# Four-layer graph network on one core: two attentions begin in another order, and the diffusion of the second is shared out as 30 and 24 products a period

## The chip, the cores and the metric

One Trainium2 chip, one core. The metric is the device time of one execution in microseconds, from the median of several runs. TensorE (PE) multiplies matrices and transposes, VectorE (DVE), ScalarE (ACT) and GpSimd (POOL) do the elementwise work and the reductions, and SyncE (SP) issues the transfers. Each engine takes its instructions in order from its own queue; they wait for each other by semaphores.

## The reference, cut to what matters

The input is `x` (3327 x 256) and a sparse weighted `adj` (3327 x 3327). Four layers follow each other, each ending in a residual and a layer norm. The change touches the last one alone:

```
def _top_p_attention(X, W1, W2, W3):
    logits = (X @ W1.T @ W2.T) @ (X @ W3.T).T
    probs = softmax(logits)
    # of each row keep the largest entries whose preceding sum is under 0.9, scale them to sum 1
    ...
R = (S + eye) / rowsum
for n in range(2):
    A  = _top_p_attention(Xa, W1, W2, W3)
    Xf = R @ Xf              # "diffusion"
    Xa = A @ Xa              # "attention"
    Z  = Z + Xf @ U1[n].T + Xa @ U2[n].T
out = layernorm(x + layernorm(X + Z))
```

The two steps of the loop are called the first and the second attention here. The second needs the result of the first for all rows, because its keys are made from all of them.

## The kernel before, in words

The rows are padded to 3328 and cut into 26 tiles of 128 (`nt` = 26, `nh` = 13). For each tile `t` of an attention there are these steps:

- `scores` (L1139 to L1164) makes the row of logits in a buffer `e` (128 x 3328). It goes in four groups: two matmuls into the PSUM tile `sc` (two banks, one buffer), then a copy to `e` by ACT. So the next group's matmuls wait for the copy of this one. One column of padding is set by a POOL memset (L1146).
- A search finds the cut of each row. `search_short` (first attention) takes the eight largest of each of 26 segments on DVE (`cand`), subtracts the maximum in an `Exp` on ACT over the whole row, ranks 48 candidates in six rounds, and zeroes what lies under the cut in two half rows (`e<-e,v` with 1664 elements). `search_long` (second attention) runs six passes of ACT over the whole row: an `Exp` at half scale (L1439), the `Exp` itself (L1444), then `Relu` (L1459) and `Sign` (L1461) at a first cut `c1`, and `Relu` (L1477) and `Sign` (L1490) at a second cut `c2`. POOL works out the cuts from the sums between the passes. With the third cut DVE masks each half row (`z`, L1506), takes segment maxima (L1356), ranks them (L1367, L1369), removes ties (L1535) and zeroes the rest in one pass over 3328 elements (L1543).
- `attended` transposes `e` on PE (`tp`, L1330), ACT copies the transposes to `wt`, and PE multiplies them with 26 blocks of `G` or `X` (L1344). For the first attention, `attended_pair` does this for two tiles at once with seven half-width products a block.
- `diffused` (second attention, L1299) multiplies 26 blocks of `adjT`, loaded in pieces `at`, with `Y`; its result `xf` lies in a ring of `DL + 3` = 4 buffers. `diffused_first` and `diffused_pair` do the same for the first attention.
- `first` ends a tile of the first attention: projections, keys and query of the second attention (`store_keys`), and one block of `G`, which is written to DRAM (`gd`) because the memory of `G` is still in use for the first attention's combinations of `X`; later it is read back. `second` ends a tile of the second attention.

In the first attention PE and DVE are held to the program's order. In the second, a scheduler orders PE's and DVE's instructions by what is ready, and ACT's passes and copies keep the program's order. The second attention is written as periods `i`: in period `i` the attention of tile `i - 1` is multiplied, tile `i` is in the last part of its search, `i + 1` in the first, and the scores of `i + 2` are made. Each period also takes a share of the 676 diffusion products:

```
later = (nt - 2) * nt
shares = [later * (k + 1) // (nt - 1) - later * k // (nt - 1) for k in range(nt - 1)]
for i in range(-2, nt + 1):
```

That is 26 in each of the periods -1 and 0, and 24 or 25 in each of the periods 1 to 25.

The first attention begins with the scores of tile 0, one group after each four products of `diffused_first`; the pair diffusion `spreading(1)` is started before tile 1's scores. The second attention begins after the last tile's `first`, in new pools.

Of the kernel before, what the change touches and what calls it, by code (L numbers as in the profile page):

```python
# [18 lines left out]
P = 128  # L19
D = 256  # L20
# [30 lines left out]
def gnn_kernel(ctx: ExitStack, tc: tile.TileContext, n: int, a: dict, out: bass.AP):  # L51
# [816 lines left out]
    with tc.tile_pool(name="l3", bufs=1) as pool, tc.tile_pool(name="l3d", bufs=1, space=DRAM) as dram:  # L868
# [269 lines left out]
        def in_order(op):  # L1138
            return lambda *x, **k: tc.keep_in_program_order(op(*x, **k))  # L1139

        def scores(work, psum, p, q, e):


            copy = in_order(nc.scalar.copy) if p else nc.scalar.copy
            if npad > n:
                nc.gpsimd.memset(e[:, n:], NEG)  # L1146
            halves = e.rearrange("p (h c) -> p h c", h=2)
            for c0 in range(0, half, KC):
                pl = psum.tile([P, 2, 512], F32, name="sc", bufs=1)
                ws = [min(KC, n - c0 - h * half) for h in range(2)]  # L1150

                for h, w in enumerate(ws):
                    k = slice(h * DA, (h + 1) * DA)
                    mm = tensor.matmul(pl[:, h, :w], q[k, :], kT[p][k, c0:c0 + w], start=True, stop=True)  # L1154
# [150 lines left out]
        def diffused(work, atp, psum, p, it, out, each=J3):  # L1305

            rd = rdeg[:, it:it + 1]
            t = work.tile([P, D], F32, name="t")
            nc.gpsimd.tensor_scalar(t, (Y if p else X)[:, it, :], rd, None, op0=ALU.mult)
            if p:  # L1310
                s = work.tile([P, D], F32, name="s")
                nc.sync.dma_start(s, sd[it])
                nc.gpsimd.tensor_tensor(t, t, s, op=ALU.add)
            for acc in aggregated(atp, psum, it, Y if p else X, each):
                if acc is None:
                    yield
            d = work.tile([P, D], F32, name="xf", bufs=DL + 3)
            nc.vector.scalar_tensor_tensor(d, acc, rd, t, op0=ALU.mult, op1=ALU.add)
            out.append(d)

# [100 lines left out]
        junks = [None]  # L1421
        edge = [None]

        def search_long(work, sm, e, total, v, kept, halves=False):

# [1 line left out]

            def t(name):  # L1430
                return t1(sm, name)

            m8, neg, root = t1(sm, "m8", 8), t1(sm, "neg", 2), t("root")
            nc.vector.max(m8, e[:, :KC])
# [22 lines left out]
            f1, sg, k1, m1 = t("fs1"), t("sg"), t("k1"), t("m1")  # L1457
# [3 lines left out]
            here(nc.scalar.activation(junk, e, AF.Sign, bias=c1, scale=-1.0, accum_out=sg))  # L1461
# [19 lines left out]
            with tc.issue_after(second_cut.ins):  # L1481
# [8 lines left out]
            here(nc.scalar.activation(junk, e, AF.Sign, bias=c2, scale=-1.0, accum_out=sg))  # L1490
            yield
            x, c3 = t("x"), t("c3")
            nc.vector.reciprocal(s, s)
# [59 lines left out]
        def first(work, psum, it, acc, f, xf, tag="pj", xa=None):  # L1553

            xa = work.tile([P, D], F32, name="h") if xa is None else xa
            nc.scalar.mul(xa, acc, f)
            yield
            pt = psum.tile([P, 4, P], F32, name=tag)
            for i, v in enumerate((xf, xa)):
                for k in range(2):  # L1560
                    tensor.transpose(pt[:, 2 * i + k, :], v[:, k * P:(k + 1) * P], ident)
            xt = work.tile([P, 4, P], F32, name="xt", bufs=1)
            vector.tensor_copy(xt, pt)
            yield
            ps = psum.tile([P, 4, P], F32, name=tag).rearrange("p (k x) d -> p k (x d)", k=2)
            for k in range(4):
                tensor.matmul(ps[:, 0, :], xt[:, k, :], (u1 if k < 2 else u2)[:, 0, k % 2, :], start=(k == 0), stop=(k == 3))
            for k in range(2):
                tensor.matmul(ps[:, 1, :], xt[:, k, :], u1[:, 1, k, :], start=(k == 0), stop=(k == 1))
            nc.scalar.copy(Y[:, it, :], ps[:, 1, :])  # L1570
            yield
            s = work.tile([P, D], F32, name="s")
            vector.tensor_add(s, ps[:, 0, :], X[:, it, :])
            nc.sync.dma_start(sd[it], s)
            pg = psum.tile([P, 4, P], F32, name=tag).rearrange("p (k x) d -> p k (x d)", k=2)
            for k in range(2):
                tensor.matmul(pg[:, 0, :], xt[:, 2 + k, :], u2[:, 1, k, :], start=(k == 0), stop=(k == 1))
            project_keys(pg[:, 1, :P], it, xt[:, 2:, :])
            g = G[:, it, :] if tag == "pj" else work.tile([P, D], F32, name="s")
            nc.scalar.copy(g, pg[:, 0, :])  # L1580
            if tag != "pj":
                nc.sync.dma_start(gd[it], g)
            store_keys(work, pg[:, 1, :P], 1, it)
            yield
# [70 lines left out]
        with tc.tile_pool(name="l3w", bufs=2) as work, tc.tile_pool(name="l3s", bufs=4) as sm:  # L1655


            def start(p, t, es, searches, search):
                if p or t:
                    q = work.tile([2 * DA, P], F32, name="q")  # L1660
                    nc.sync.dma_start(q, qd[p][t])
                else:
                    q = q0
                es[t] = work.tile([P, npad], F32, name="e", bufs=4)
                searches[t] = search(work, sm, es[t], *(x[p][:, t:t + 1] for x in (tots, vs, kepts)),
                                     **({"halves": True} if p and t == nt - 1 else {}))
                return scores(work, psum, p, q, es[t])

            with tc.tile_pool(name="l3p", bufs=2, space=PSUM) as psum, tc.tile_pool(name="l3a", bufs=1) as quads:
                fixed = True  # L1670
# [56 lines left out]
                        next(todo[r][0])  # L1727
                    ends[0] = todo[0][0]

                groups = logits(0)  # L1730
                x = diffused_first(quads, psum, 1, xfs)
                for _ in groups:
                    next(x)
                queue.append(searches[0])
                spread = spreading(1)
                groups = logits(1)
                for _ in x:
                    next(groups, None)
                    looks(2)
                for _ in groups:  # L1740
                    pass
                queue.append(searches[1])
# [2 lines left out]
                for i in range(nh - 1):  # L1745
                    stage(spread, 7, logits(2 * i + 2), ends, counts,
                          {0: lambda: end_pair(i - 1) if i else None, 5: lambda: attend_to(i), 6: go_on})
                    go_on()
                    counts = [1, 2, 2, 2, 2, 0, 0]
                    queue.append(searches[2 * i + 2])  # L1750
                    values = turned[0]
                    for k in range(7):
                        next(values)
                        looks(k in (1, 2, 4, 5, 6))
                    stage(spread, 6, logits(2 * i + 3), todo[1], [2, 1, 2, 1, 2, 1], {})
                    finish()
# [14 lines left out]
                for it in (nt - 2, nt - 1):  # L1771
# [14 lines left out]
                        pass  # L1786
                    ends = first(quads, psum, it, acc, f, xfs[it], "tp", c)
                    next(ends)
                both(ends)
                fl0 = unresolved(sm, psum, 0)  # L1790
                fixed = False
            for x in (slice(0, JH), slice(JH, nt)):
                nc.sync.dma_start(G[:, x, :], gd[x].rearrange("t p d -> p t d"))

            with tc.tile_pool(name="l3q", bufs=3, space=PSUM) as psum, tc.tile_pool(name="l3at", bufs=3) as atp, \
                    tc.tile_pool(name="l3b", bufs=2) as lone:
                es, searches, xfs = {}, {}, []  # L1800
                result = iter(())
                spread = (x for j in range(nt) for x in diffused(lone, atp, psum, 1, j, xfs, 1))
                later = (nt - 2) * nt
                shares = [later * (k + 1) // (nt - 1) - later * k // (nt - 1) for k in range(nt - 1)]
                for i in range(-2, nt + 1):
                    def search(t):
                        if 0 <= t < nt:
                            next(searches[t])
# [6 lines left out]
                    share = iter(range(shares[i - 1] if 0 < i < nt else nt if -2 < i < 1 else 0))  # L1815

                    def diffuse(products):
                        for _ in range(products):
# [192 lines left out]
```

## Time and profile before

| | us |
|---|---|
| median of 3 runs (3396.72 to 3399.24) | 3396.89 |
| the profiled execution, its own time | 3392.58 |
| its span | 3390.8 |
| busy: PE / DVE / ACT / POOL | 3121.1 / 2692.5 / 1730.8 / 1133.6 |
| first attention's scores begin / second attention's scores begin | 1697.9 / 2547.7 |
| first transposes of the second attention's tile 0 | 2617.1 |

The profiled execution is 1.8 us longer than its span and 4.3 us shorter than the median. "Busy" is an engine's time in instructions; a busy PE is not a PE at its peak. A row of the timeline gives the start in us from the span's start, the duration, engine, line, operation, output and inputs with their shapes, how often in sequence, and in square brackets how long the engine stood idle before it and what ended that.

### The profile page before, as it was taken

The page shows a single profiled execution, that of the slowest core. Times are in us where ns is not written, and L with a number is a line of the kernel's source. Part 1 is how long each engine was busy: PE and PEld are TensorE (multiplying, and loading weights), DVE is VectorE, ACT ScalarE, POOL GpSimd, SP SyncE. Part 2 cuts the span into 40 slices and gives each one's busy share as a digit, 9 for nine tenths or more (in the row PEclk, how much of TensorE's full clock was granted, in tenths as well). Part 3 has the DMA queues.
Part 4 walks back from the last instruction along what each step waited for, and adds up shares of the span by engine and source line. Part 5 has one row for each costly group of instructions (what it writes and reads, how often), then busy time and mean ns, then how long its engine had stood idle before and what let it go on. Part 6 is the DMA issues. An engine that isn't in the chain of part 4 may idle for free. (4 is left out here: it accounts for less than half of the span.)

```text
span 3390.8 us, 50286 instructions
## 1 busy us (share of the span) xinstructions
PE 3121.1 (92%) x18301; PEld 2560.0 (75%) x18301; DVE 2692.5 (79%) x5899; ACT 1730.8 (51%) x2763; POOL 1133.6 (33%) x1328
## 2 busy tenths in 40 slices
PE   8999888988888766999979999999997899999997
PEld 5999656666676555888858898898885677777776
DVE  4665268999999998777578878878854899999996
ACT  1000556767667676111133433433436888888883
POOL 0000245656666655111220000000003566666663
PEclk9999999998999888999989999999998999999999
DMA  6775334333343221444322322322313122222221
GB/s 200 250 257 191 112 98 121 114 108 110 103 118 98 63 61 46 167 143 151 118 79 85 89 73 81 89 73 81 89 41 108 42 68 69 66 59 73 72 63 35
DMA packets 206264, 344.31 MB, mean 102 GB/s; under 512 B 22222, under 2 KB 129166, under 8 KB 205870
## 3 DMA queue, kind: packets, MB, share of 16 engines
q1 hardware_dynamic: 205998, 340.92, 33.1%
q8 instruction: 148, 2.42, 0.3%
q14 instruction: 118, 0.97, 0.1%
HBM read 304.65 MB, written 36.21 MB: 101 GB/s over the span
## 5 line engine op out<-in xcount | busy, mean ns | idle before, releaser
L330 POOL TENSOR_TENSOR h<-du,row 128x2048 f32<-128x2048 f32 (+1 forms) x110 | 465.9, 4235 | 344.7 <-DVE hc L330 243.0
L330 DVE TENSOR_TENSOR_SCAN h<-dA,carry,h 128x512 f32<-128x512 f32 (+1 forms) x384 | 448.8, 1221 | 21.7 <-ACT dA L337 21.5
L337 ACT ACTIVATE dA<-t,A_log 128x512 f32<-128x512 f32 (+1 forms) x448 | 292.6, 658 | 147.7 <-DVE h L330 146.0
L1299 PE MATMUL acc<-F,at 128*128 128x256 f32 x1352 | 345.4, 384 | 3.0 <-DMA at<-in_adjT 2.1
L1344 PE MATMUL acc<-G,wt 128*128 128x256 f32 x1352 | 332.6, 388 | 8.6 <-ACT wt L1139 8.3
L1079 PE MATMUL acc<-F,at 128*128 128x257 f32 x1352 | 302.1, 380 | 0.8 <-ACT r L1023 0.8
L389 PE MATMUL cb<-F,at 128*128 128x256 f32 x1196 | 293.0, 393 | 7.6 <-ACT hn L409 3.4
L1344 PEld LDWEIGHTS acc<-G,wt 128*128 128x128 f32 x1352 | 248.9, 191 | 65.3 <-ACT wt L1139 35.5
L1299 PEld LDWEIGHTS acc<-F,at 128*128 128x128 f32 x1352 | 241.8, 191 | 53.6 <-issue 21.5
L1079 PEld LDWEIGHTS acc<-F,at 128*128 128x128 f32 x1352 | 252.4, 190 | 36.1 <-issue 1.1
L680 PE MATMUL y<-ident,hc 128*128 128x128 f32 x1664 | 235.9, 296 | 45.7 <-DVE hc L330 45.5
L1146 POOL MEMSET e<- 128x1 f32 x52 | 4.9, 99 | 816.2 <-PE tp L891 752.5
L680 PEld LDWEIGHTS y<-ident,hc 128*128 128x128 f32 x1664 | 209.4, 153 | 86.6 <-DVE hc L330 62.1
L389 PEld LDWEIGHTS cb<-F,at 128*128 128x128 f32 x1196 | 228.7, 197 | 58.8 <-issue 20.4
L330 DVE TENSOR_TENSOR hc<-h,row 128x2048 f32<-128x2048 f32 (+2 forms) x114 | 243.0, 2133 | 9.7 <-PE y L680 2.6
L891 PE MATMUL acc<-X,at 128*128 128x128 f32 (+1 forms) x988 | 173.7, 287 | 6.1 <-issue 6.1
L1263 ACT COPY wt<-tp 128x512 f32<-128x512 f32 x156 | 90.7, 591 | 167.1 <-PE tp L891 151.7
L138 PE MATMUL acc<-t,cb 128*128 128x128 f32 (+1 forms) x1014 | 168.4, 275 | 0.0
L891 PEld LDWEIGHTS acc<-X,at 128*128 128x128 f32 x988 | 142.3, 194 | 30.1 <-issue 25.3
L891 PE MATMUL acc<-G,sw 128*128 128x128 f32 x936 | 155.5, 275 | 0.0
L1160 ACT COPY e<-sc 128x832 f32<-128x832 f32 x78 | 65.9, 845 | 174.8 <-PE sc L891 174.7
L891 DVE MAX8 cand<-e 128x8 f32<-128x128 f32 x676 | 139.8, 278 | 5.5 <-ACT e L1160 3.7
(417 smaller groups left out, 7273.0 us busy)
## 6 DMA issues: line engine op xcount, KB each, us to landing
at<-in_adjT SPq DMA_DIRECT2D x54, 832.0 KB, 4.4
at<-in_adjT SPq DMA_DIRECT2D x130, 320.0 KB, 3.0
row<-bc SPq DMA_DIRECT2D x80, 512.0 KB, 4.9
at<-in_adjT SPq DMA_DIRECT2D x52, 640.0 KB, 5.3
at<-in_adjT SPq DMA_DIRECT2D x52, 576.0 KB, 4.3
at<-in_adjT SPq DMA_DIRECT2D x72, 256.0 KB, 3.1
at<-mixed SPq DMA_DIRECT2D x72, 256.0 KB, 3.6
mixed<-cb SPq DMA_DIRECT2D x26, 640.0 KB, 3.9
```

The lines of the kernel that those rows point to most:

```text
L138: mm = nc.tensor.matmul(acc, w[:, j, :], x, start=(y == 0 and k % 3 == 0 and k < 6), stop=(y == nh - 1 and k in (2, 6)))
L330: return lambda *x, **k: tc.keep_in_program_order(op(*x, **k))
L337: decays.append(op(*x, **k))
L389: ten.matmul(acc, at[:, j % JC, :], X0[:, j, :], start=(j == 0), stop=(j == nt - 1))
L680: x = ten.matmul(y[:, g * P:(g + 1) * P], h[:, g, i * P:(i + 1) * P], ident, is_transpose=True, start=(first and g == 0), stop=(last and g ...
L891: return lambda *x, **k: tc.keep_in_program_order(op(*x, **k))
L1079: nc.tensor.matmul(acc, at[:, j, :], F[:, j0 + j, :], start=(j0 + j == 0), stop=(j0 + j == nt - 1))
L1146: nc.gpsimd.memset(e[:, n:], NEG)
L1160: copy(halves[:, :, c0:c0 + ws[0]], pl[:, :, :ws[0]])
L1263: nc.scalar.copy(wts[-1], pt)
L1299: nc.tensor.matmul(acc, at[:, j, :], rhs[:, j0 + j, :], start=(j0 + j == 0), stop=(j0 + j == nt - 1))
L1344: tensor.matmul(acc, wt[:, j, :], rhs[:, j0 + j, :], start=(j0 + j == 0), stop=(j0 + j == nt - 1))
```

## The change

It has five parts.

1. Beginning of the first attention. `scores` may use several PSUM tiles in turn: for tile 0 these are `sc` and one of the `acc` buffers. All four groups of tile 0 come ahead of `diffused_first`. Tile 1's scores are interleaved with `diffused_first` at every second step, with three looks at the search in each step. `spreading(1)` comes after that loop. A one-element ACT copy `ex` is added.
2. End of the first attention. The last four tiles' blocks of `G` are written straight into `G`. The other 22 are read back before the last pair's ends, no longer after all.
3. Beginning of the second attention. The scores of tile 0 are made inside the last `first`, two steps in each of its three. An explicit list of steps for tiles 0 and 1 takes the place of periods -2 and -1.
4. Tile 0 of the second attention is `counted`: its two `Sign` passes on ACT become four `tensor_scalar` passes over half rows on DVE (`is_gt`, summed), two for each cut, with an addition and a rescaling of one column.
5. The shares of diffusion become 30 products in each of periods 1 to 4 and 24 in each of periods 5 to 25. The ring of `xf` has 5 buffers.

```diff
-            for c0 in range(0, half, KC):
-                pl = psum.tile([P, 2, 512], F32, name="sc", bufs=1)
+            for k, c0 in enumerate(range(0, half, KC)):
+                bank = banks[k % len(banks)]
+                pl = psum.tile([P, 2, 512], F32, name=bank, bufs=1 if bank == "sc" else 2)
...
-            d = work.tile([P, D], F32, name="xf", bufs=DL + 3)
+            d = work.tile([P, D], F32, name="xf", bufs=DL + 4)
...
+            def signs(c):
+                ks, sg = t1(sm, "ks", 2), t("sg")
+                if counted:
+                    for h in range(2):
+                        z = lone.tile([P, half], F32, name="z", bufs=1)
+                        nc.vector.tensor_scalar(z, e[:, h * half:(h + 1) * half], c, 0.0, op0=ALU.is_gt, op1=ALU.add,
+                                                accum_out=ks[:, h:h + 1])
+                    nc.vector.tensor_add(sg, ks[:, :1], ks[:, 1:])
+                    nc.vector.tensor_scalar(sg, sg, -2.0, float(npad), op0=ALU.mult, op1=ALU.add)
+                else:
+                    here(nc.scalar.activation(junk, e, AF.Sign, bias=c, scale=-1.0, accum_out=sg))
+                return sg
...
-            g = G[:, it, :] if tag == "pj" else work.tile([P, D], F32, name="s")
+            direct = tag == "pj" or it >= nt - 4
+            g = G[:, it, :] if direct else work.tile([P, D], F32, name="s")
...
-                groups = logits(0)
+                nc.scalar.copy(small.tile([P, 1], F32, name="ex"), eps_t)
                 x = diffused_first(quads, psum, 1, xfs)
-                for _ in groups:
-                    next(x)
+                for _ in logits(0):
+                    pass
                 queue.append(searches[0])
+                groups = logits(1)
+                for k, _ in enumerate(x):
+                    if k % 2 == 0:
+                        next(groups, None)
+                    looks(3)
                 spread = spreading(1)
-                groups = logits(1)
-                for _ in x:
-                    next(groups, None)
-                    looks(2)
...
+                for x in (slice(0, JH), slice(JH, nt - 4)):
+                    nc.sync.dma_start(G[:, x, :], gd[x].rearrange("t p d -> p t d"))
                 end_pair(nh - 2)
...
-                both(ends)
+                es, searches = {}, {}
+                groups = start(1, 0, es, searches, search_long)
+                for _ in ends:
+                    next(groups)
+                    next(groups)
+                both(groups)
...
-            for x in (slice(0, JH), slice(JH, nt)):
-                nc.sync.dma_start(G[:, x, :], gd[x].rearrange("t p d -> p t d"))
...
-                later = (nt - 2) * nt
-                shares = [later * (k + 1) // (nt - 1) - later * k // (nt - 1) for k in range(nt - 1)]
-                for i in range(-2, nt + 1):
+                later, tail = (nt - 2) * nt - 4 * (nt + 4), nt - 5
+                shares = 4 * [nt + 4] + [later * (k + 1) // tail - later * k // tail for k in range(tail)]
+                groups = start(1, 1, es, searches, search_long)
+                for t, products in ((0, 0), (0, 0), (None, 0), (None, 4), (0, 0), (None, 0), (None, 4),
+                                    (0, 0), (0, 0), (None, 0), (None, 4), (0, 0), (None, 0), (None, 4),
+                                    (0, 0), (1, 0), (1, 4), (0, 0), (0, 6)):
+                    next(groups if t is None else searches[t], None)
+                    for _ in range(products):
+                        next(spread)
+                for i in range(nt + 1):
```

More of the change, by code (lines that the diff above doesn't have):

```diff
@@ L1139, in in_order, with scores @@
             return lambda *x, **k: tc.keep_in_program_order(op(*x, **k))
-        def scores(work, psum, p, q, e):
+        def scores(work, psum, p, q, e, banks=("sc",)):
             copy = in_order(nc.scalar.copy) if p else nc.scalar.copy
@@ L1422, in gnn_kernel, with search_long @@
         edge = [None]
-        def search_long(work, sm, e, total, v, kept, halves=False):
+        def search_long(work, sm, e, total, v, kept, halves=False, counted=False):
             def t(name):
                 return t1(sm, name)
+            def signs(c):
[10 more added lines that the diff above has]
+                return sg
             m8, neg, root = t1(sm, "m8", 8), t1(sm, "neg", 2), t("root")
@@ L1456, in search_long @@
             inverse(rc, c1)
-            f1, sg, k1, m1 = t("fs1"), t("sg"), t("k1"), t("m1")
+            f1, k1, m1 = t("fs1"), t("k1"), t("m1")
             yield
@@ L1460, in search_long @@
             yield
-            here(nc.scalar.activation(junk, e, AF.Sign, bias=c1, scale=-1.0, accum_out=sg))
+            sg = signs(c1)
             yield
@@ L1489, in search_long @@
                 scaled(level, c2, float(npad), level, ALU.mult, ALU.add)
-            here(nc.scalar.activation(junk, e, AF.Sign, bias=c2, scale=-1.0, accum_out=sg))
+            sg = signs(c2)
             yield
@@ L1578, in first @@
             project_keys(pg[:, 1, :P], it, xt[:, 2:, :])
-            g = G[:, it, :] if tag == "pj" else work.tile([P, D], F32, name="s")
+            direct = tag == "pj" or it >= nt - 4
+            g = G[:, it, :] if direct else work.tile([P, D], F32, name="s")
             nc.scalar.copy(g, pg[:, 0, :])
-            if tag != "pj":
+            if not direct:
                 nc.sync.dma_start(gd[it], g)
@@ L1665, in start @@
                 searches[t] = search(work, sm, es[t], *(x[p][:, t:t + 1] for x in (tots, vs, kepts)),
-                                     **({"halves": True} if p and t == nt - 1 else {}))
-                return scores(work, psum, p, q, es[t])
+                                     **({"halves": t == nt - 1, "counted": t == 0} if p else {}))
+                return scores(work, psum, p, q, es[t], ("sc", "acc") if not p and t == 0 else ("sc",))
             with tc.tile_pool(name="l3p", bufs=2, space=PSUM) as psum, tc.tile_pool(name="l3a", bufs=1) as quads:
@@ L1788, in gnn_kernel @@
                     next(ends)
-                both(ends)
+                es, searches = {}, {}
[4 more added lines that the diff above has]
+                both(groups)
                 fl0 = unresolved(sm, psum, 0)
                 fixed = False
-            for x in (slice(0, JH), slice(JH, nt)):
-                nc.sync.dma_start(G[:, x, :], gd[x].rearrange("t p d -> p t d"))
             with tc.tile_pool(name="l3q", bufs=3, space=PSUM) as psum, tc.tile_pool(name="l3at", bufs=3) as atp, \
                     tc.tile_pool(name="l3b", bufs=2) as lone:
-                es, searches, xfs = {}, {}, []
+                xfs = []
                 result = iter(())
                 spread = (x for j in range(nt) for x in diffused(lone, atp, psum, 1, j, xfs, 1))
-                later = (nt - 2) * nt
-                shares = [later * (k + 1) // (nt - 1) - later * k // (nt - 1) for k in range(nt - 1)]
-                for i in range(-2, nt + 1):
+                later, tail = (nt - 2) * nt - 4 * (nt + 4), nt - 5
[8 more added lines that the diff above has]
+                for i in range(nt + 1):
                     def search(t):
@@ L1814, in gnn_kernel @@
                         logits = start(1, i + 2, es, searches, search_long)
-                    share = iter(range(shares[i - 1] if 0 < i < nt else nt if -2 < i < 1 else 0))
+                    share = iter(range(shares[i - 1] if 0 < i < nt else nt if i < 1 else 0))
                     def diffuse(products):
```

## The prediction, written before the result

> **What bounds the kernel now.** I read the page first: engines' sums, then the 40 slices.
>
> ```profile
> PE 3121.1 (92%) x18301; PEld 2560.0 (75%) x18301; DVE 2692.5 (79%) x5899; ACT 1730.8 (51%) x2763; POOL 1133.6 (33%) x1328
> ...
> PE   8999888988888766999979999999997899999997
> ...
> PEclk9999999998999888999989999999998999999999
> ```
>
> PE is the bound, except in a few slices. Two of the dents are the change's places: the slices about 1700-1780 (a 7) and about 2540-2630 (7, 8). In the table by stage (PE, PEld, DVE, ACT and POOL busy, clock, DMA share, GB/s) they look like this, with two settled stretches below:
>
> ```profile
> 1740.00:1750.00 10.00, 2.58 (x20) 1.81 (x16) 9.20 (x37) 4.23 (x4) 0.00 (x0) 0.88 0.41 123
> 1750.00:1760.00 10.00, 7.35 (x37) 6.10 (x38) 5.91 (x12) 2.54 (x6) 0.00 (x0) 0.60 0.03 8
> 2550.00:2560.00 10.00, 7.08 (x17) 2.08 (x16) 0.25 (x1) 4.83 (x5) 2.84 (x4) 0.50 0.93 315
> 2610.00:2620.00 10.00, 2.90 (x11) 2.50 (x12) 9.89 (x17) 4.08 (x5) 4.43 (x2) 0.56 0.07 27
> ...
> 3220.00:3240.00 20.00, 20.00 (x102) 15.32 (x101) 19.23 (x66) 15.96 (x18) 12.73 (x30) 1.00 0.18 51
> 3240.00:3260.00 20.00, 20.00 (x97) 14.15 (x96) 18.20 (x54) 16.71 (x17) 14.25 (x22) 1.00 0.20 66
> ```
>
> At both starts PE stands still while DVE or ACT searches tile 0; late in the second attention PE is full. So time at the starts is worth its face value, provided PE's order behind them is the same work; in the build it is (from tile 2's scores on in the first attention the orders agree; before the transposes of the second's tile 0 there are 75 products of diffusion instead of 78).
>
> **First attention's start.** The timeline:
>
> ```profile
> 1716.18 0.18 POOL L1146 MEMSET e<- 128x1 f32 x4
> 1720.70 3.07 ACT L1407 ACTIVATE e<-e,neg 128x3328 f32<-128x3328 f32 x1 [3.73 <-DVE neg L891]
> 1726.72 0.49 DVE L891 SCALAR_TENSOR_TENSOR F<-acc,rdeg,F 128x256 f32<-128x256 f32 x1 [5.79 <-PE acc L891]
> 1737.48 5.12 DVE L891 MAX8 cand<-e 128x8 f32<-128x128 f32 x26
> 1751.31 0.45 PE L891 MATMUL tp<-ident,e 128*128 128x128 f32 x1 [8.73 <-DVE e L891]
> ```
>
> Before, three of tile 0's four groups lie behind diffusion products that wait for `at`; `e` is whole at 1717.0, the maxima end at 1720.0, `Exp` runs 1720.7-1723.8. Then DVE stands 5.79 for `diffused_first`, and its in-order queue holds tile 1's maxima and tile 0's cut behind that, so the first transposes wait to 1751.3. After, the four groups in two PSUM tiles need no product: `e` about 1704.3. But the last column of padding comes from POOL's memset, which runs at 1716.18 because POOL works off 23 own-part products first (1690.0-1716.2, unchanged). So 25 maxima are early and the 26th is not: maximum 1716.6, `Exp` 1717.3-1720.6, cut 1723.0-1726.8. The DVE block is thereby covered; tile 1's maxima start at about 1729.6 (-7.9), the pair diffusion at 1728.2, its 12.65 us are unchanged, and transposes come at about 1743 (-8). Without the memset I would have written 11-13.
>
> PE's clock: 1750-1760 was granted 0.60, about 2 us lost over the first products after the wait of 8.73. The Trainium skill ("TensorE: Matmul & The Clock Gate", "Part 1: The HAM clock gate") has the clock fall after an idle window of about 3.4 us; my new waits there are 2.3 and 1.6, so by the rule PE stays warm: gain 10. Against it stands 2550-2560, at 0.50 with no PE wait over 2.3 in or just before it: gain 8 (the whole sum 30 or 28). Taken: **9** (bounds 4-14: no overlap gained beyond the earlier `Exp`, or that plus the whole DVE wait and the clock). The copy `ex` costs nothing and brings nothing: in the build it stands in an earlier layer, and the table load before the first score copy is still there.
>
> **Second attention's start.**
>
> ```profile
> 2547.71 0.97 PE L1154 MATMUL sc<-kT,q 64*128 64x416 f32 x4 [2.28 <-ACT q L907]
> 2554.99 1.75 PE L1154 MATMUL sc<-kT,q 64*128 64x416 f32 x4 [0.95 <-ACT e L1139]
> 2557.79 3.07 ACT L1439 ACTIVATE junk<-e,neg 128x3328 bf16<-128x3328 f32 x1
> 2573.51 3.09 ACT L1461 ACTIVATE junk<-e,c 128x3328 bf16<-128x3328 f32 x1
> 2585.12 3.07 ACT L1490 ACTIVATE junk<-e,c 128x3328 bf16<-128x3328 f32 x1
> 2590.38 1.95 DVE L1506 SCALAR_TENSOR_TENSOR z<-e,c 128x1664 f32<-128x1664 f32 x1
> 2617.10 1.97 PE L1330 MATMUL tp<-ident,e 128*128 128x128 f32 x8 [9.20 <-DVE e L1543]
> 2639.78 3.54 POOL L1447 TENSOR_SCALAR c<-c,more,less 128x2 f32<-128x2 f32 x1
> ```
>
> - Scores earlier: they ran 2547.7-2556.7, about 2.7 us a group. Three groups move into the last `first`, whose PE waits cover them; the fourth needs the last keys (copied to 2547.4) and ends about 2549. First `Exp` 2550.0 instead of 2557.8: **-7.8**. The last four blocks of `G` skip their DRAM write; L1580 waited 2.33 for one, part of this.
> - Read-back of `G` (1.66 MB), issued at 2548.94 ahead of the `at` loads, moves before the last pair's ends. In SP's queue it then stands behind the 22 writes that it needs, and the last pair's stores and the loads of `s` and `at` stand behind it: if a write were late, these would be too, by some 2-3 us (the `at` loads land 3-5 us after their issue). I take nothing, since those 22 blocks were written tens of us before. PE waits for the read-back only in tile 0's attention, 40 us later. `at` lands at about 2553.8; first products were at 2559.4.
> - Two `Sign` passes (3.07 and about 0.19 for the sum, each) leave ACT's queue; with tile 0 alone they were on the chain (Relu, Sign, POOL, Relu, Sign). Four DVE passes of 1664 run beside `Relu`. Nearest row: the 1664-element `z`, 1.95, so 3.9 a cut. The Trainium skill ("VectorE: DVE Perf Modes", "Mode 2×_2P") lets a one-source fp32 operation in SBUF do two elements a cycle: 2.0 a cut. The trace is against it: `L97 TENSOR_SCALAR` 128x256 has a mean of 404 ns, two-source forms of that width 425. By either the sum is the same, since `Relu`'s result comes 0-3 us later than the sums; if accumulating cost double, 3.9 more a cut would show, some 5 in all.
> - But tile 1's `Exp` half now stands before tile 0's second `Relu` in ACT's order: +3.1 given back, partly in the POOL wait that was there (2.05). `z` starts at 2574-2576 instead of 2590.4: -14 to -16.
> - The cut: 26.7 us from `z` to its end, with 2.03 of waiting for POOL that I expect to shrink, while an `xf` and a reciprocal of tile 1 come in between (+0.7). Transposes at about 2600 instead of 2617: **-16** (13-18; POOL's `c` took 3.54 instead of some 0.3 when it met L1543, and this can befall the new DVE passes, twice).
>
> **Shares 30/24.** A product is 0.433 us (four in 1.73). Periods, by the distance of their transposes: 26.1, 33.5, 31.0, 30.6, 30.3, 30.9, 28.7, 29.5, later ones 29.9 on average. PE's own sum of a period: 51 products 22.1, transposes 2.8, scores 3.6, so 28.5 and about 1 of waits. One product less in each of 19 periods (5 to 23) is at most 8.2; DVE at 27.2 and ACT at 25.5 a period leave room for it, but waits return some: 6.5. The two last periods gain 0.4. Periods 2 to 4 take 28, 30 and 30 instead of 11, 25 and 25 in PE's order; period 2 has about 9 us of PE waits that 17 products (7.4) fill, at a cost of 0.5-1.5; periods 3 and 4, with little wait left, +0.8 and +1.1. Net **-4** (bounds -6 to +3: below nothing if the waits are longer than PE's sum says and one product less shortens nothing). The fifth `xf` buffer only permits this. Ends and tail are unchanged, 0.
>
> Sum: 9 + 16 + 4 = 29. The profiled execution takes 3392.6, so 3363.6; it stands 4.3 under the median of the runs, which gives 3396.9 - 29 = **3368**.
>
> **Rivals.**
> 1. The starts pay only in part and the split nothing: the memset and the second cut's wait pin tile 0; `Exp` earlier by 3.4 at the first start, 10 at the second, split 0: 13, thus 3384. For it: in-order DVE and POOL queues, each with one late item. Against: the waits of 5.79, 2.28 and 2.33 have releasers that the change moves.
> 2. More: the clock stays warm at both starts (2 each) and the split gives its 8 without return: 10 + 20 + 9 = 39, thus 3358. Against it: that row of 0.50, and the returns named above.
> 3. Slower: in the second attention POOL's cut `c` meets DVE's full pass L1543, as at 2639.78, in each period rather than in some. ACT's second `Relu` waits for that `c`, and behind it in ACT's program order the `wt` copies that PE's products need. The price is up to 3.2 us in each of 24 periods; it decides from (9 + 16 + 4)/24 = 1.2 a period. At 1.6 the time is 3397 + 9 = 3406. For it: the new order of steps shifts phases for good. Against: the program's steps within a period are the same, and ACT has 4 us of slack in each.
> 4. The change not doing what it says holds for `ex`, in the build already.
>
> **How the numbers follow.** The sum's own case 0.56 (3360-3376); rival 1, 0.18; rival 2, 0.12; rival 3, 0.11; about nothing 0.03. From no change a measurement of this kernel tells about 0.2%, 7 us. Faster by more: 0.86; within: 0.03; slower: 0.11. The range reaches from 3354, beyond rival 2, to 3388, beyond rival 1; outside it lie rival 3 and the ends.
>
> **What would show it.** The first attention's first transposes of `e` at 1743, not 1751; its `Exp` at about 1717.3, released by the maximum over the memset's column. The second's first `Exp` at 2541 and tile 0's transposes near 2591 on the new clock of the trace (9 subtracted). DVE passes of 1664 near 1.95 (or 1.0), and `Relu` ending later than they. Periods of 29.1-29.2 from the fifth on. Wrong: transposes of tile 0 earlier by less than 10, periods at 30 or above, a new wait of ACT or PE for `c`, or `at` loads behind the read-back of `G`.

## The result and the profile after

The changed kernel takes 3373.99 us (median of 5 runs, 3371.27 to 3379.68) against 3396.89. The ratio is 0.9942, with a 95% interval of 0.993 to 0.9955, so 15 to 24 us faster. The forecast was 3368, with a range of 3354 to 3388. The profiled execution took 3371.27, with a span of 3369.5, 21.3 less than before.

Not all of these 21.3 belong to the change. The layers ahead of it are the same in both kernels, and yet this POOL row, the last one before the first attention, starts 2.9 us earlier (timeline of POOL: start, duration, engine, line, operation; first before, then after):

```profile
1688.79 1.23 POOL L1098 TENSOR_SCALAR X<-o,mv,rs 128x256 f32<-128x256 f32 x1
```
```profile
1685.89 1.23 POOL L1098 TENSOR_SCALAR X<-o,mv,rs 128x256 f32<-128x256 f32 x1
```

In all the profiles of this case the row starts somewhere between 1684.87 and 1693.13, whatever the edit behind it. It serves as the zero below. From it to the end the kernel before took 1702.0, the changed one 1683.6: the change is worth 18.4 in these two traces. The page of the changed kernel, its engines' sums and slices:

```profile
PE 3118.6 (93%) x18301; PEld 2560.5 (76%) x18301; DVE 2701.4 (80%) x5911; ACT 1723.3 (51%) x2760; POOL 1128.0 (33%) x1328
...
PE   8999888988888766899989999999999999999997
...
PEclk9999998999999888999999999999999999999999
```

The two dents at the beginnings are mostly filled. The table by stage shows it in numbers (PE, PEld, DVE, ACT and POOL busy, clock, DMA share, GB/s), and the one stretch that is new, in the last row:

```profile
1740.00:1750.00 10.00, 8.73 (x58) 6.28 (x57) 8.10 (x18) 3.47 (x7) 0.00 (x0) 0.91 0.24 69
1750.00:1760.00 10.00, 10.00 (x92) 10.00 (x92) 8.24 (x32) 3.17 (x7) 0.00 (x0) 1.00 0.02 5
2550.00:2560.00 10.00, 10.00 (x46) 7.25 (x44) 6.25 (x12) 7.64 (x7) 4.20 (x15) 1.00 0.37 104
2590.00:2600.00 10.00, 9.48 (x46) 6.97 (x46) 9.82 (x28) 4.92 (x5) 1.42 (x4) 0.92 0.13 36
...
2710.00:2720.00 10.00, 5.95 (x19) 3.78 (x17) 2.80 (x13) 6.48 (x5) 4.44 (x15) 0.73 0.03 8
```

To see where the time went, each trace is cut at the same events: the zero; the last copy of a query (L907), which ends the first attention; the starts of the cuts of tiles 0, 6, 23 and 24 of the second attention (the full DVE pass `e<-e,v`, L1543 before, L1557 after); the end. All in us:

| | zero to last query | to cut 0 | to cut 6 | to cut 23 | to cut 24 | to the end | sum |
|---|---|---|---|---|---|---|---|
| before | 858.6 | 66.0 | 182.3 | 503.3 | 32.6 | 59.3 | 1702.0 |
| changed | 851.5 | 51.9 | 187.6 | 499.8 | 32.8 | 59.9 | 1683.6 |
| difference | -7.1 | -14.0 | +5.3 | -3.5 | +0.3 | +0.6 | -18.4 |

The beginnings brought 21.1, the late periods 3.5, and six early periods gave 5.3 back. The periods, from cut to cut, are 26.3, 30.6, 29.2, 30.4, **37.7**, **33.5** and then 29.4 each, more or less; before, they were 26.1, 33.5, 31.0, 30.6, 30.3, 30.9 and then 29.6 on average. Periods 4 and 5 (numbered by the tile whose cut opens them; the kernel's own number is one higher) are what has to be explained.

The rows of period 4 in the changed kernel, from the timelines of POOL, DVE, ACT and PE in this order:

```profile
2704.05 0.73 POOL L1606 TENSOR_TENSOR t<-X,ln_b 128x256 f32<-128x256 f32 x1 [6.14 <-DVE xf L1319]
2704.86 0.19 POOL L1461 TENSOR_SCALAR k<-sg 128x1 f32<-128x1 f32 x1
2705.86 3.81 POOL L1461 TENSOR_SCALAR na<-m,lim,rc 128x1 f32<-128x1 f32 x1
2711.42 0.34 POOL L1461 TENSOR_SCALAR c<-c,more,less 128x2 f32<-128x2 f32 x1
...
2705.86 3.69 DVE L1557 SCALAR_TENSOR_TENSOR e<-e,v 128x3328 f32<-128x3328 f32 x1
...
2712.87 0.16 DVE L1507 RECIPROCAL s<-s 128x1 f32<-128x1 f32 x1 [3.32 <-POOL s L1461]
...
2711.79 3.07 ACT L1491 ACTIVATE junk<-e,c 128x3328 bf16<-128x3328 f32 x1 [4.58 <-POOL c L1461]
...
2715.26 2.07 PE L1345 MATMUL acc<-G,wt 128*128 128x256 f32 x4 [4.05 <-ACT wt L1139]
```

Read from the top: POOL waits 6.14 for DVE's `xf`, to write `X + ln_b` into a buffer of `t`. Behind this row in its queue stand the steps of the next tile's second cut (`k`, `na`, `c`), whose input, the `Sign` pass on ACT, had ended at 2701.5. So they begin 3.4 late. Then `na` starts in the same moment as DVE's cut pass and takes 3.81 instead of 0.34. ACT's second `Relu` waits 4.58 for `c`, the `wt` copies stand behind it, and PE waits 4.05; the granted clock falls to 0.73. In the kernel before, at the same cut, POOL had no wait for `xf`, `c` was out in time, and one DVE row stood elsewhere:

```profile
2732.61 0.34 POOL L1447 TENSOR_SCALAR c<-c,more,less 128x2 f32<-128x2 f32 x1
...
2734.32 0.15 DVE L1493 RECIPROCAL s<-s 128x1 f32<-128x1 f32 x1
2734.44 3.68 DVE L1543 SCALAR_TENSOR_TENSOR e<-e,v 128x3328 f32<-128x3328 f32 x1
```

This reciprocal needs the next tile's `s`, which POOL makes after `c`. Ahead of the cut pass it keeps DVE from starting the pass before `c` is out; in the changed kernel the scheduler placed it behind.

### The profile page after: what moved, and what is told of

The parts are those of the page before. It is cut to its first block, busy times and chain, and to the rows that moved or that the text cites. A ratio compares the mean times of both kernels' runs of the same rounds, so it can differ in the third digit from the quotient of the medians.

```text
span 3369.5 us, 50288 instructions
## 1 busy us (share of the span) xinstructions
PE 3118.6 (93%) x18301; PEld 2560.5 (76%) x18301; DVE 2701.4 (80%) x5911; ACT 1723.3 (51%) x2760; POOL 1128.0 (33%) x1328
## 4 chain that ended last, share of the span: by engine, by line
PE 42%; ACT 7%; DVE 5%; POOL 4%; issue 1%; DMA 1%; SPq 0%; DVEq 0%; ACTq 0%; POOLq 0%
PE acc L891 15%; PE acc L1079 8%; PE tp L891 6%; PE acc L1345 4%; ACT junk L1444 3%; PE acc L1300 3%; PE sc L891 3%; ACT junk L1491 2%; PE sc L1155 2%; PE tp L1331 1%; DVE cand L1357 1%; ACT e L1139 1%; ACT wt L1139 1%; DVE z L1520 1%; DVE e L1549 1%
## 5 line engine op out<-in xcount | busy, mean ns | idle before, releaser
L891 PEld LDWEIGHTS acc<-X,at 128*128 128x128 f32 x988 | 142.6, 194 | 26.1 <-issue 23.2
L1444 ACT ACTIVATE junk<-e,c 128x3328 bf16<-128x3328 f32 x50 | 154.2, 3083 | 0.0
```

Of the source, the lines that this page charges most:

```text
L1444: here(nc.scalar.activation(junk, e, AF.Sign, bias=c, scale=-1.0, accum_out=sg))
```

## The experiments

The medians of one kernel scatter by some us, so each verdict rests on the sections of the trace first, one trace for each kernel. "To last query" differs by up to 1.7 between traces of kernels whose first beginning is the same, so a difference of that size says nothing. "Sum" is from the zero to the end: 1702.0 before, 1683.6 changed. Ratios are against the kernel before on the same chip. Those of the single edits to the changed kernel below overlap its 0.993 to 0.9955, so there the sections alone speak.

**The parts alone.** In `e_first` the first beginning alone, in `e_second` the second (with the direct blocks of `G` and the fifth `xf` buffer), in `e_split` the shares and the fifth `xf` buffer alone; `e_even` is the changed kernel without the split, but with the fifth buffer:

```diff
-                later, tail = (nt - 2) * nt - 4 * (nt + 4), nt - 5
-                shares = 4 * [nt + 4] + [later * (k + 1) // tail - later * k // tail for k in range(tail)]
+                later = (nt - 2) * nt
+                shares = [later * (k + 1) // (nt - 1) - later * k // (nt - 1) for k in range(nt - 1)]
```

> The kernel before with the beginning of the first attention alone changed (two PSUM tiles for tile 0's scores, all four groups ahead, pair diffusion later). Theory (the parts add up): the last key copy of the first attention comes at 2537.5 to 2538.5 instead of 2547.4, since in the changed kernel it came at 2537.39 and the direct blocks of G can have given at most a little of that; the whole time falls by 8 to 10. Rival (the second beginning swallows part of it, because its first scores waited for something else): under 6.

> The changed kernel with the first attention's beginning as before and even shares of diffusion (24 and 25): the second attention's beginning alone. Theory: tile 0's cut starts 14 us earlier than before (2599 to 2600 instead of 2613.4), and the whole time falls by 10 to 14. Rival (the gain of the beginning is given back in the next four or five periods whatever the shares are, since the later tiles' searches set their pace): the cut is 14 earlier, the time falls by under 6.

> The kernel before with the shares 30 and 24 and the fifth xf buffer alone. My prediction had -4. Theory (the long stretch of 37.65 + 33.46 us in periods 4 and 5 of the changed kernel comes from where the shares of 30 put the end of a tile's diffusion, on which POOL's queue then waits): the stretch is found here too, the other periods are 29.4 instead of 29.9, and the time changes by -2 to +4. Rival (the stretch comes from the new beginning): no period over 34 after the third, time -6 to -8.

> The changed kernel with even shares of diffusion (24 and 25): everything but the split. Theory as for the shares alone: no stretch of 37 in period 4, later periods 29.5 to 29.9, so the time is 3370 to 3376, as with the split within 4 us. Rival (30 products early pay because they fill idle PE time): 3378 to 3382, slower than the changed kernel by over 4.

| | to last query | to cut 0 | to cut 6 | to cut 23 | sum | gain | median, ratio (95%) |
|---|---|---|---|---|---|---|---|
| `e_first` | 851.8 | 65.9 | 182.4 | 503.5 | 1695.3 | 6.7 | 3383.34, 0.9975 (0.9963-0.9987) |
| `e_second` | 858.2 | 51.7 | 185.5 | 503.4 | 1691.4 | 10.6 | 3379.75, 0.9957 (0.9942-0.9971) |
| `e_split` | 857.4 | 67.3 | 183.1 | 499.9 | 1699.7 | 2.3 | 3389.25, 0.9982 (0.9971-0.9992) |
| `e_even` | 852.0 | 53.4 | 183.8 | 503.1 | 1684.9 | 17.1 | 3371.89, 0.9933 (0.9912-0.9954) |

The two beginnings add up (6.7 + 10.6 = 17.3, together 17.1). The second one reaches its 14.3 at cut 0 and gives 3.2 back by cut 6. The split is worth 2.3 alone (by its ratio 3 to 10), of which 1.2 lies ahead of the last query, where it changes nothing, and 1.3 on top (1684.9 - 1683.6), which is within the scatter; the medians of these two don't part either. My expectation for `e_split` was wrong in one thing: its longest early period is 34.5, in period 1, and the stretch of 37.7 is not there; nor is it in `e_even` (longest 34.2). So neither shares nor beginning make it alone. The traces show what each gives. At cut 4 of `e_split` POOL waits for `xf` as in the changed kernel, but the reciprocal stands ahead of the pass:

```profile
2729.22 0.73 POOL L1591 TENSOR_TENSOR t<-X,ln_b 128x256 f32<-128x256 f32 x1 [6.14 <-DVE xf L1318]
...
2734.58 0.16 DVE L1493 RECIPROCAL s<-s 128x1 f32<-128x1 f32 x1 [3.59 <-POOL s L1447]
```

In `e_even` and `e_second`, with even shares, POOL has no wait for `xf` at this cut (their longest is 5.0, two periods earlier). The wait at this cut comes with the shares, then, and the stretch needs DVE's changed order as well.

The expectation for `e_first` (8 to 10; 6.7 came) counted absolute times from the span's start, which held the 2.9 and more of the layers ahead.

**POOL's queue, first try.** A buffer of its own for `X + ln_b`:

```diff
-            xb = work.tile([P, D], F32, name="t")
+            xb = work.tile([P, D], F32, name="xb", bufs=1)
```

> The changed kernel, where POOL's product of the residual (X + ln_b, L1606) gets a buffer of its own instead of the ring of two that it shares with the diffusion's own part. In the changed kernel it waited 6.14 us for DVE's xf in period 4, the second cut of the next tile stood behind it in POOL's queue, came 3.3 us late, and one of its steps then took 3.81 instead of 0.34 beside DVE's pass L1557; ACT waited 4.58 and PE 4.05. Theory: period 4 falls from 37.65 to 29.5 to 31 and period 5 from 33.5 to about 30, cut 0 to cut 6 takes 176 to 179 instead of 187.6, and the time is 8 to 11 us under that of the changed kernel. Rival (POOL's step would meet the DVE pass anyway, with the phase of the periods): a stretch over 33 remains in one of the periods 1 to 6, gain under 4.

Nothing was won: sum 1683.2, period 4 38.8, ratio 0.9938 (0.9919 to 0.9956). The timeline of POOL says why:

```profile
2694.88 0.73 POOL L1606 TENSOR_TENSOR xb<-X,ln_b 128x256 f32<-128x256 f32 x1
2704.92 0.94 POOL L1310 TENSOR_SCALAR t<-F,rdeg 128x256 f32<-128x256 f32 x1 [7.18 <-DVE xf L1319]
...
2706.77 3.69 POOL L1461 TENSOR_SCALAR k<-sg 128x1 f32<-128x1 f32 x1
```

`xb` no longer waits, but the next user of the freed ring, L1310, now stands in the same place in POOL's order, and it waits for the same `xf`. The wait was renamed, not removed, so this run did not test the theory. `e_both` below shows the same period (38.8).

**POOL's queue, second try.** The instruction is moved behind the next tile's `lim` in POOL's order; the orders of the other engines stay as they are:

```diff
-            nc.gpsimd.tensor_tensor(xb, X[:, it, :], b3, op=ALU.add)
+            if it == nt - 1: nc.gpsimd.tensor_tensor(xb, X[:, it, :], b3, op=ALU.add)
...
             with tc.issue_after(edge[0].ins) if edge[0] else nullcontext():
-                power(rs, mv)
+                nc.gpsimd.tensor_tensor(xb, X[:, it, :], b3, op=ALU.add); power(rs, mv)
```

> The changed kernel, where POOL's product X + ln_b, alone, is issued later in POOL's order: after the next tile's lim (L1469) and not ahead of the second cut's steps. The orders of PE, DVE, ACT and SP are those of the changed kernel. (With a buffer of its own, another POOL instruction, the diffusion's own part L1310, took its place and waited 7.18 us for the same xf.) Theory: nothing in POOL's queue waits for xf ahead of the cut any more; period 4 falls from 37.65 to 29.5 to 31, cut 0 to cut 6 from 187.6 to 177 to 180, and the time by 8 to 11. Rival (DVE is too far ahead of ACT here, its pass L1557 meets the cut's steps in any case): period 4 stays above 33, gain under 4.

Period 4 fell from 37.7 to 32.2 and period 5 from 33.5 to 30.6; cut 0 to cut 6 took 180.4. The sum is 1677.7, 5.9 under the changed kernel; ratio 0.992 (0.9899 to 0.994). POOL, DVE and ACT in the same period:

```profile
2707.64 0.19 POOL L1461 TENSOR_SCALAR k<-sg 128x1 f32<-128x1 f32 x1 [2.63 <-ACT junk L1444]
2708.64 0.34 POOL L1461 TENSOR_SCALAR na<-m,lim,rc 128x1 f32<-128x1 f32 x1
2710.73 0.34 POOL L1461 TENSOR_SCALAR c<-c,more,less 128x2 f32<-128x2 f32 x1
...
2712.96 3.68 DVE L1557 SCALAR_TENSOR_TENSOR e<-e,v 128x3328 f32<-128x3328 f32 x1
...
2713.59 3.07 ACT L1491 ACTIVATE junk<-e,c 128x3328 bf16<-128x3328 f32 x1
```

Now POOL waits for its real input, `na` takes 0.34, and `c` is out 1.9 before DVE's pass: ACT's `Relu` has no wait behind it. DVE's order is that of the changed kernel, reciprocal behind the pass, so the wait for `xf` was needed for the stretch. The gain was less than I had written (8 to 11): in period 3 DVE waits 1.65 instead of 0.77 for POOL's `h` (L1628), which comes later for the moved row; in period 4 PE is busy 29.85 of the 30 us from 2700 to 2730; and the last period grew from 32.8 to 34.0.

**Tile 0 counted on ACT.** The changed kernel with the two `Sign` passes back on ACT:

```diff
-                                     **({"halves": t == nt - 1, "counted": t == 0} if p else {}))
+                                     **({"halves": t == nt - 1, "counted": False} if p else {}))
```

> The changed kernel, where tile 0 of the second attention counts with its two Sign passes on ACT, as all other tiles do. Theory: from the last query copy to tile 0's cut it takes 5 to 6 us longer than the 51.9 of the changed kernel (two passes of 3.07 on ACT's chain, some of it hidden in waits for POOL), and the whole time is longer by up to as much. Rival (tile 0's cut does not matter, since the next tiles set the pace): the cut is later, the time is not.

Cut 0 came only 2.8 later (54.8), and cut 6 was 5.0 earlier: cut 0 to cut 6 took 180.0 instead of 187.6. Sum 1678.7, ratio 0.9925 (0.9906 to 0.9944). Neither expectation had this sign: the part meant to shorten the chain made the kernel 4.9 slower in the trace. POOL's rows in the period that corresponds, then DVE's:

```profile
2710.74 0.73 POOL L1606 TENSOR_TENSOR t<-X,ln_b 128x256 f32<-128x256 f32 x1 [6.13 <-DVE xf L1319]
...
2714.68 0.34 POOL L1461 TENSOR_SCALAR c<-c,more,less 128x2 f32<-128x2 f32 x1
...
2716.20 3.73 POOL L1461 TENSOR_SCALAR high<-c,double 128x1 f32<-128x1 f32 x1
...
2716.13 0.16 DVE L1507 RECIPROCAL s<-s 128x1 f32<-128x1 f32 x1 [3.62 <-POOL s L1461]
2716.21 3.67 DVE L1557 SCALAR_TENSOR_TENSOR e<-e,v 128x3328 f32<-128x3328 f32 x1
```

The wait for `xf` is the same, 6.13. But here `Sign` ended 8.1 before DVE's pass (2708.1 to 2716.2) and not 4.4 (2701.5 to 2705.9), so `c` was out when the pass began, and the blocked row is `high`, which is wanted later. These 4 us are not a lead of DVE over ACT: DVE had done the work ahead of its pass 4.4 after `Sign` in both kernels (2712.5 here, 2705.8 there). They are the 3.62 for which the reciprocal, ahead of the pass again, waits for POOL's `s`. So counting tile 0 on DVE gave the stretch through the place of one DVE row, four tiles later. The runs agree with this: the stretch of 37.7 or more is in the four that at cut 4 have both POOL's wait of 6 to 7 and the reciprocal behind the pass (the changed kernel, `e_xb`, `e_memset`, `e_both`), not in the three with the wait alone (`e_split`, `e_acts`, `e_am`), nor in the two with that order alone (`e_late`, `e_latem`). The changed kernel with that row alone moved was not run.

**The padding column.** The changed kernel with the column of tile 0 of the first attention set by DVE:

```diff
-                nc.gpsimd.memset(e[:, n:], NEG)
+                (vector if len(banks) > 1 else nc.gpsimd).memset(e[:, n:], NEG)
```

> The changed kernel, where the padding column of tile 0 of the first attention is set by DVE ahead of the maxima and not by POOL behind 20 own parts. In the changed kernel the last maximum waited 3.22 us for it. Theory: the maxima end at about 1710.3 instead of 1713.5 (same zero), the exponential starts 3 earlier, the copy behind it too, PE's wait of 4.43 falls to about 1.3, and the first transposes come 2.5 to 3.2 earlier; whole time -2.5 to -3.5. Rival (the pair diffusion's loads, for which DVE waited 2.84, are the next bound): first transposes under 1.5 earlier.

In the changed kernel, at this place, DVE, ACT and PE read so (timeline):

```profile
1713.04 0.18 POOL L1146 MEMSET e<- 128x1 f32 x4
1713.17 0.29 DVE L891 MAX8 cand<-e 128x8 f32<-128x128 f32 x1 [3.22 <-POOL e L1146]
...
1714.18 3.07 ACT L1408 ACTIVATE e<-e,neg 128x3328 f32<-128x3328 f32 x1 [7.78 <-POOL F L1204]
...
1718.13 1.75 PE L891 MATMUL sc<-kT,q 64*128 64x416 f32 x4 [4.43 <-ACT e L1161]
1719.82 5.23 PE L891 MATMUL acc<-X,at 128*128 128x256 f32 x12
...
1729.01 0.69 DVE L891 TENSOR_TENSOR cb<-at 128x512 f32<-128x512 f32 x1 [2.84 <-DMA at<-mixed]
...
1738.10 0.64 PE L891 MATMUL acc<-G,cb 128*128 128x128 f32 x2 [3.08 <-DVE cb L891]
...
1743.59 0.49 PE L891 MATMUL tp<-ident,e 128*128 128x128 f32 x3
1745.22 0.33 PE L891 MATMUL tp<-ident,e 128*128 128x128 f32 x1 [1.15 <-DVE e L891]
```

With the edit (zero 0.9 later) PE's waits are shorter:

```profile
1715.70 0.97 PE L891 MATMUL sc<-kT,q 64*128 64x416 f32 x4 [1.02 <-ACT e L1161]
1716.60 2.86 PE L891 MATMUL acc<-X,at 128*128 128x256 f32 x12
...
1738.82 0.30 PE L891 MATMUL tp<-ident,e 128*128 128x128 f32 x1 [1.08 <-DVE e L891]
```

The exponential starts 3.4 earlier, the last query comes 5.5 earlier (846.0), more than the 3 expected. The rest fits the clock: it was granted at 0.77 in 1720-1730 of the changed kernel, after the wait of 4.43 (the same four score matmuls take 1.75 instead of 0.97, the twelve matmuls behind them 5.23 instead of 2.86), and at 1.00 in all of 1700-1750 with the edit. But the way to cut 0 grew by 1.1 to 53.0 and that from cut 0 to cut 6 to 189.5, and the sum is 1681.0: 2.6 of 5.5 are left. Ratio 0.993 (0.9913 to 0.9948).

**Edits together.** `e_both` has the own buffer and the column, `e_am` the column and `Sign` on ACT, `e_latema` the moved POOL row too, `e_latem` the moved row and the column with tile 0 counted on DVE.

> The changed kernel with both edits, POOL's residual in a buffer of its own and the padding column set by DVE. Theory: the gains add up, 11 to 14 us under the changed kernel, a median of about 3358 to 3362. Rival: as for each alone.

> The changed kernel with tile 0's Sign passes on ACT as for all tiles, and the padding column of the first attention's tile 0 set by DVE. Alone, by the trace from the same zero before the first attention to the end, they took 4.9 and 2.6 us off. Theory: the column's 5.5 at the first beginning and the 4.9 add up, 10 under the changed kernel: from the zero to the end 1672 to 1674 instead of 1683.6, a median of about 3363 to 3367. Rival (the second attention's phase shifts with the earlier beginning): a stretch of over 33 comes back in periods 3 to 6.

> As the kernel before it in this list (Sign on ACT for tile 0, padding column on DVE), and POOL's X + ln_b issued later. There POOL waited 6.1 us in period 3 too, but DVE came later and the second cut was out before its pass. Theory: period 3 of 32.7 falls to 30 to 31, 1 to 3 us more. Rival (the wait on POOL is free there, since the cut's steps were done in time): within 1 us of the kernel before it.

> The changed kernel (tile 0 counting on DVE) with two edits: POOL's X + ln_b issued later, and the padding column of the first attention's tile 0 set by DVE. By the trace, from the zero to the end, they took 5.9 and 2.6 off alone, the second one with 5.5 at its own place and 1.9 given back later, in the stretch of periods 1 to 6 that the first one removes. Theory: 1672 to 1675 from the zero to the end instead of 1683.6; median 3362 to 3367, as fast as the two kernels with Sign on ACT. Rival (the earlier beginning shifts the phase again): a period over 34 before the last, over 1677.

| | to last query | to cut 0 | to cut 6 | longest of periods 1 to 6 | sum | median, ratio (95%) |
|---|---|---|---|---|---|---|
| `e_both` | 847.4 | 52.0 | 187.2 | 38.8 | 1679.0 | 3374.81, 0.9935 (0.9912-0.9958) |
| `e_am` | 845.7 | 55.8 | 180.5 | 32.7 | 1674.6 | 3366.39, 0.9915 (0.9898-0.9931) |
| `e_latema` | 846.2 | 54.5 | 179.8 | 32.0 | 1674.9 | 3365.70, 0.9910 (0.9893-0.9926) |
| `e_latem` | 846.0 | 52.9 | 181.5 | 32.3 | 1674.4 | 3362.92, 0.9900 (0.9883-0.9916) |

`e_both` brought 4.6 of the 11 to 14 expected, since the own buffer does nothing. `e_am` brought 9.0 of its 10.4 (5.5 and 4.9). With `Sign` on ACT the moved row changes nothing (its rival was right): period 3 falls from 32.7 to 30.3, period 4 grows from 28.9 to 32.0. All of the last three are faster than the changed kernel by their sections, by about 9 of 1683.6, and two of them, with `e_latem` the lowest, also by intervals that lie apart from 0.993-0.9955. Which of the three is the best the runs do not tell.

## Why the prediction was right, and where it was not

The direction, the places and the range held; the sum was 29, the medians show 22.9 and the traces 18.4. By the prediction's own steps:

- **First beginning, -9: measured -7.1.** The maximum did wait for the memset's column and the exponential started 3.6 earlier, as written. The transpose that waits for the end of tile 1's cut came 5.0 earlier (59.3 after the zero instead of 64.3), not 8. The step that failed is the start of tile 1's maxima, written as 1729.6: on that clock it was 1732.5 (1729.62 plus 2.9), since DVE waited 2.84 for the pair diffusion's `mixed` load ahead of them. Also missed: score copies of tile 1 stand behind the exponential in ACT's order, a new PE wait of 4.43 with a slower clock after it. The clock term was right: 1750-1760 is at 1.00 instead of 0.60, and from that transpose to the first product with `wt` PE took 4.5 instead of 6.3 for the same matmuls, 1.9 of the other 2.1. The price of the memset was put too low: 2 to 4 in the text (11-13 less 9), 5.5 at its place in `e_memset`. The transpose, in the kernel before (after it is in the fence of the padding column):

```profile
1753.10 0.48 PE L891 MATMUL tp<-ident,e 128*128 128x128 f32 x1 [1.33 <-DVE e L891]
```

- **Second beginning, -16: measured -14.0 to cut 0.** From the last query to the first `Exp` 3.2 instead of 10.4, so -7.2 (written: -7.8); to the first `z` 28.7 instead of 43.0, so -14.3 (written: -14 to -16). What did not come is the shorter cut: from `z` to the cut pass 23.2 instead of 23.0. The row for the `z` pass was the right one for counting (next fence), and the cover was right: neither half pass was waited for beyond `Relu`.

```profile
L1439 DVE TENSOR_SCALAR_CACHE_REDUCE z<-e,c 128x1664 f32<-128x1664 f32 x4 | 7.8, 1946 | 6.6 <-POOL c L1461 6.6
```

- **Shares, -4: measured +2.1 from cut 0 to cut 24** against before, of which the second beginning with even shares makes +1.3 and the split +0.9 (2.0 won ahead of cut 0 leave it the 1.3 above). Alone, in `e_split`, it gave -2.4 there, not far from the -4. Two terms were mis-sized. One product less in each late period gave 3.5 over 17 periods, 0.2 each, half of what a product takes: these periods are 29.4, not 29.1. (The 29.9 from which the prediction starts has the last period's 32.6 in it, the others are 29.7; and 29.9 less its own 0.34, 6.5 over 19, is 29.6, not 29.1 to 29.2.) And the cost of the first periods, put at 2.4 to 3.4, did not have the stretch of 8 + 4.
- **The third rival's mechanism was real, its extent not.** I had POOL's cut meeting DVE's pass in each of 24 periods. It met it in two, 4 (at `na`, ahead of `c`) and 5 (there `c` took 3.60); in most others the pass blocked a POOL row that stands behind `c`. I had the price, 3.54 at 2639.78, in front of me and looked for it in the wrong term: at tile 0, where the rows before showed it, not where 30 products would make POOL wait for `xf`, nor in what the new steps would do to DVE's order.
- The tail was written as unchanged and grew by 0.6, as in every run with the new second beginning (59.8 to 60.1) and in none without (59.3); why was not tried. `ex` did nothing, as written. The read-back of `G` held up neither `at` nor `s` by a visible amount at the start of the second attention.

## What to carry to other kernels

Price an edit at the place where it works, then read what it does to the order of the queues behind it: taking two passes off ACT for one tile also moved one DVE row, and so DVE's long pass onto POOL's short steps, and cost 4.9 net in the trace. When an engine is late, look in its queue for the row ahead that waits for something else, and move that row; a further buffer can just let another row take its place. Where layers ahead of a change wander by some us, set a zero behind them in each trace and compare sections.

## What the runs showed of the hardware

- A POOL step of one or two columns in these rows takes 0.2 to 0.4 alone and 3.5 to 3.8 when DVE's pass of 3.69 with two inputs from SBUF is running (`na` 3.81, `c` 3.54, `high` 3.73): it ends with the pass. Beside DVE's counting pass, with one input, POOL's `rc` kept its 0.57 (2548.18, in 2548.06-2550.0). The Trainium skill says this ("SBUF — State Buffer", "Who interferes with whom"): a DVE instruction with two inputs in SBUF locks out a POOL instruction that reads there. The prediction had the row and not the rule, and so feared the counting passes at tile 0 beside the cut pass; `rc` shows no lock there.
- PE's clock after waits, in these stages: waits of 1.0 to 2.5 us left it at 1.00 throughout (`e_memset`, 1710-1750); 4.43 brought 0.77 in the ten us behind it, and after 3.08 a pair of matmuls took 0.64 instead of 0.39. The row of 0.50 without a wait over 2.3, which the prediction held against the rule, has a companion in the changed kernel: 2540-2550 at 0.66, with no wait of PE over 1.7. Single waits don't explain these two; what does stays open.
- The counting form of `tensor_scalar` over 1664 fp32 elements took 1.946, as long as the two-input `z` pass (1.963). No faster mode was seen.
